# Graph attention on one core: batch 0's self_feat as seven block products, and the value blocks cleared and copied in two groups

## The chip, the core and the metric

The kernel runs on one core of a Trainium2 chip. The core has five engines with queues of their own: PE (TensorE; PEld are its weight loads), DVE (VectorE), ACT (ScalarE), POOL (GpSimd) and SP (SyncE, which here only issues DMAs; POOL and ACT issue a few as well). Each engine works through its instructions in the order in which they were written, and waits on semaphores for what the others have to deliver. The metric is the device time of one execution in microseconds (us). A difference of two kernels is told from runs on the same chip.

## The reference, cut to what matters

There are 16 batches of 512 rows with 512 features. Every row attends to the first 20 rows of its batch, with 16 heads, in two directions `d`:

```python
self_feat = concat([v, q_exp]) @ W_self.T + b_self          # q_exp is 0 where a row of v sums to 0
for d in range(2):
    A  = (adj if d == 0 else adj.swapaxes(1, 2))[:, :, :20, :]        # 11 labels
    vb = A @ w_bias + b_bias
    kv = self_feat[:, :20]
    qh, kh = self_feat @ Wq.T + bq, kv @ Wk.T + bk                    # 16 heads of 32
    aff = where(A.sum(-1) > 0, qh . kh / sqrt(32), -9e15) + vb
    out = out + (softmax(aff) @ kv) @ Wout + bout                     # per head
return v + relu(self_feat + out)
```

## The kernel before, in words

All numbers are fp32. Features lie on partitions (`C` = 4 chunks of 128), rows along the free dimension. The query projection is folded into the keys: `keys` computes `Wq` times the keys once, so that scores are self_feat times these folded keys. `Wout` is folded into the values in the same way by `values`.

**Setup** (lines 458 to 764). After the key projections (`key_rows`) come 22 bursts of `keys`. A burst is a group of matmuls into both buffers of the PSUM pool `ps_s`, which ACT (line 689) and DVE (line 691) evict into staging tiles `st`; SP writes these to `g_d` and `g1_d` in DRAM, and batch 0's part to `g0`. Between two bursts TensorE does one entry of `plan` (line 719), a filler: `v` and `w` are steps of `values`, `c` is `bias_scores`, `n` is `row_flags`, `s` a quarter pass of `self_feat(0, ...)`. Entry 0 follows burst 4, and so on. `values` ends with a copy by DVE and DMAs issued by POOL into `vw_d` (line 657). `bias_scores(0)` also has POOL clear a tile `c` (line 628) into which ACT then copies (line 630).

**self_feat.** For batches 1 to 15 it is built from 2 x 2 blocks with seven products instead of eight (`product`, line 249): POOL forms four sums of x (`x_sum`) and, once, four sums of the weights (`weight_sums`); DVE reads the partial accumulators (`partial`, line 284) into scratch tiles `u1` to `u3` and adds them to the other products (`joined`, line 297). Product n of batch b + 1 runs during batch b. Batch 0 uses the plain form: `self_feat(0, f, h)` makes one quarter, in eight steps, and `self_copy` adds the row flags times the query part. Three quarters are made in the setup; the last one, (1, 1), stands in tile 1 of batch 0 (line 873), ahead of that tile's scores.

**Main loop** (lines 786 to 984): 16 batches of four tiles `nt` of 128 rows. Per tile TensorE does `scores`. DVE does `weigh` (adds the mask terms of `full_add`, takes the maximum, subtracts), ACT the exponent (`expo`), DVE and POOL `normal`, DVE `turn` (a transpose). `full_add` and `x_sum` are POOL's. In tile 2 of the next batch `attend(b - 1)` multiplies the turned weights with the value blocks `vd`, and `finish` adds self_feat. The masks of batch b + 1 are made on the way: `mask_mul` on ACT (eleven activations), `mask_count` and `mask_sum` on DVE, `mask_spread` on ACT. `row_sum(b + 2, j)` on ACT sums the rows of x for the flags; `new_self(b + 1)`, a small ACT copy, opens the self_feat tile of the next batch. Both stand in tile 3.

**Value blocks.** `vd` must be block diagonal. So `clear_blocks` writes zeros over `bd_d` in DRAM with one DMA, in tile 1 of batch 0, and `blocks` copies the values of all 16 batches from `vw_d` into it with twelve DMAs, in tile 2 of batch 0. `load_values(b)` then reads one batch's block: batch 0's in tile 3 of batch 0, the others in tile 0 of the next batch.

**Order.** All of it is written out by hand (`manual_schedule`). SP's DMAs are one queue; `behind(dma, instruction)` makes one wait for an instruction of another engine, and those after it wait as well. A DMA also waits for the one eight places ahead of it, as they share eight semaphores.

Of the kernel before, what the change touches and what calls it, by code (L numbers as in the profile page):

```python
# [13 lines left out]
P = 128  # L14
# [4 lines left out]
def gat_kernel(  # L19
# [64 lines left out]
    vw_d = dram.tile([2, C, BM, P], F32, name="vw_d")  # L84
    bd_d = dram.tile([C, B, 32, HL, 2, DH], F32, name="bd_d")
# [5 lines left out]
    adds, fulls, wts, outs, held, sf_ps, conds, prods = {}, {}, {}, [], [None] * 3, {}, {}, {}  # L91
    sums, parts, us, done = {}, {}, {}, {}
# [42 lines left out]
    def load_values(b, ins=None):  # L135

        vds[b] = gp.tile([P, HL, 2, DH], F32, tag="vd", name=f"vd{b}", bufs=1)
        for c in range(C):
            behind(nc.sync.dma_start(
                vds[b][bass.ts(c, 32)].rearrange("p e i g -> p (e i g)"), bd_d[c, b].rearrange("r e i g -> r (e i g)")  # L140
            ), ins if c == 0 else None)

    def clear_blocks(zero):

        nc.sync.dma_start(
            bd_d.rearrange("c b r e i g -> (c b r) (e i g)").rearrange("(n p) w -> p n w", p=P),
            zero.unsqueeze(1).to_broadcast([P, C * B * 32 // P, HL * 2 * DH]),
        )

    def blocks():  # L150

        bb = bd_d.rearrange("c b r e i g -> (c b) r e i g")
        vv = vw_d.rearrange("d c (b m) (e g) -> d (c b) m e g", m=NG, e=HL)
        for e in range(HL):
            for i in range(2):
                j = (e * S) // 32 + i
                for d in range(2):
                    lo = max(e * S + d * NG, 32 * j)
                    hi = min(e * S + (d + 1) * NG, 32 * j + 32)
                    if lo < hi:  # L160
                        m, r = lo - e * S - d * NG, lo - 32 * j
                        nc.sync.dma_start(bb[:, r : r + hi - lo, e, i], vv[d, :, m : m + hi - lo, e])


# [29 lines left out]
    def self_feat(b, f, h, parts=((0, range(C)), (1, range(C)))):  # L194


        lo, hi = max(NG, h * N // 2), (h + 1) * N // 2
        for i, ks in parts:
            if (i, ks[0]) == (0, 0):
                if (f, h) == (0, 0):  # L200
                    new_self(b)
                held[0] = bank(f"ps_sf{b}_{f}{h}", 3 if (f, h) == (1, 1) else None)
            for k in ks:
                for a in range(HL):
                    nc.tensor.matmul(  # L205
                        held[0][bass.ts(a, R), i * N // 2 : i * N // 2 + hi - lo],
                        ws_v[:, k, bass.ds((2 * f + i) * P + a * R, R)], xs[b][:, k, lo:hi],
                        start=(k == 0), stop=(k == C - 1),
                    )
            if (i, ks[-1]) == (1, C - 1):  # L210
                sf_ps[b, f, h] = held[0]

    def self_copy(b, f, h):

        lo, hi = max(NG, h * N // 2), (h + 1) * N // 2
        ps = sf_ps.pop((b, f, h))
        for i in range(2):
            nc.vector.scalar_tensor_tensor(
                sfs[b][:, 2 * f + i, lo:hi], nzs[b][:, lo:hi], qw[:, 2 * f + i, b : b + 1],
                ps[:, i * N // 2 : i * N // 2 + hi - lo], ALU.mult, ALU.add,  # L220
            )

# [15 lines left out]
    def x_sum(b, n):  # L238

        t = sums[b, n] = xsum.tile([P, 2, HN], F32, tag=f"t{n}", name=f"t{b}_{n}")  # L240
# [8 lines left out]
    def product(b, n):  # L249
# [11 lines left out]
        if n == 1:  # L261
            parts[b, "a"] = [bank(f"ps_a{b}_{i}", i) for i in range(2)]
        if n == 2:
            parts[b, "d"] = bank(f"ps_d{b}", 2)
        if n == 5:
            parts[b, "c"] = bank(f"ps_c{b}", 3)
# [30 lines left out]
    def joined(b, n, key, f, l):  # L297
# [769 lines left out]
```

## Time and profile before

| | us |
|---|---|
| median of 3 runs | 587.78 (587.18 to 588.13) |
| profiled execution, its own time | 586.05 |
| its span, first to last instruction | 583.9 |
| PE busy, share of the span | 575.7 (99%) |
| DVE busy | 489.0 (84%) |
| ACT busy | 395.6 (68%) |
| POOL busy | 384.9 (66%) |

Setup is the time up to the first scores at 91.38 us; a batch in the middle of the loop takes some 30.5 us. In rows of the chain, numbers are the start, the length and the piece of work; in rows of a timeline, start, length, engine, line, operation, tiles and shapes, and in brackets the idle time of the engine ahead of it and what ended it ("issue": nothing that the profile shows). In the trace TensorE has two records for each matmul, so that 16 matmuls are "x32". Ends of matmuls are modelled. A row of a DMA is its issue on SP or POOL.

### The profile page before, as it was taken

The page shows a single profiled execution, that of the slowest core. Times are in us where ns is not written, and L with a number is a line of the kernel's source. Part 1 is how long each engine was busy: PE and PEld are TensorE (multiplying, and loading weights), DVE is VectorE, ACT ScalarE, POOL GpSimd, SP SyncE. Part 2 cuts the span into 40 slices and gives each one's busy share as a digit, 9 for nine tenths or more (in the row PEclk, how much of TensorE's full clock was granted, in tenths as well). Part 3 has the DMA queues.
Part 4 walks back from the last instruction along what each step waited for, and adds up shares of the span by engine and source line. Part 5 has one row for each costly group of instructions (what it writes and reads, how often), then busy time and mean ns, then how long its engine had stood idle before and what let it go on. Part 6 is the DMA issues. An engine that isn't in the chain of part 4 may idle for free.

```text
span 583.9 us, 30310 instructions
## 1 busy us (share of the span) xinstructions
PE 575.7 (99%) x13184; PEld 437.0 (75%) x13184; DVE 489.0 (84%) x783; ACT 395.6 (68%) x1162; POOL 384.9 (66%) x351
## 2 busy tenths in 40 slices
PE   9999999999999999999999999999999999999996
PEld 6654547887878787877878787787887878787873
DVE  0485565889898989899999999898989898989895
ACT  1334644586877777868686868687786877777671
POOL 2405663648778685858586777686868677776775
PEclk9999999999999999999999999999999999999999
DMA  8999899857766675757576767676676765664404
GB/s 303 388 407 311 331 377 320 273 123 213 209 197 196 185 214 169 217 167 217 168 214 171 214 171 212 177 199 188 199 202 187 199 198 172 199 199 114 144 15 146
DMA packets 103220, 124.14 MB, mean 213 GB/s; under 512 B 21712, under 2 KB 71920, under 8 KB 101040
## 3 DMA queue, kind: packets, MB, share of 16 engines
q1 hardware_dynamic: 101296, 119.79, 66.8%
q8 instruction: 104, 1.70, 1.3%
q0 software_dynamic: 672, 1.36, 1.0%
q10 hardware_dynamic: 1120, 1.06, 0.5%
q14 instruction: 28, 0.23, 0.2%
HBM read 82.30 MB, written 40.24 MB: 210 GB/s over the span
## 4 chain that ended last, share of the span: by engine, by line
PE 98%; DVE 0%; issue 0%; ACT 0%; DVEq 0%
PE ps_s L365 46%; PE ps_a L282 17%; PE ps_c L282 9%; PE ps_o L435 6%; PE ps_d L282 4%; PE ps_v L649 3%; PE ps_k L586 3%; PE ps_sf L205 2%; PE ps_kv L537 2%; PE ps_o L779 1%; PE ps_warm L496 1%; PE ps_nz L189 0%; PE ps_s L354 0%; PE ps_c L622 0%; PE ps_q L547 0%
## 5 line engine op out<-in xcount | busy, mean ns | idle before, releaser
L365 PEld LDWEIGHTS ps_s<-g,sf 128*32 128x32 f32 x8192 | 262.8, 110 | 20.9 <-issue 13.0
L365 PE MATMUL ps_s<-g,sf 128*32 128x152 f32 x8192 | 276.7, 293 | 0.5 <-ACT st L689 0.5
L337 ACT COPY both<-add 32x80 f32<-32x80 f32 x512 | 130.8, 256 | 53.8 <-DVE add L328 48.0
L417 POOL TENSOR_TENSOR s<-s,sm 128x640 f32<-128x640 f32 x63 | 80.4, 1276 | 94.2 <-DVE sm L416 68.2
L344 POOL TENSOR_TENSOR full<-cq,both 128x640 f32<-128x640 f32 x64 | 100.4, 1568 | 27.5 <-issue 21.3
L317 ACT ACTIVATE prod<-adj,wb_sb 128x80 f32<-128x80 int32 x330 | 112.4, 433 | 0.0
L392 ACT ACTIVATE s<-s 128x640 f32<-128x640 f32 x63 | 46.5, 738 | 64.1 <-DVE s L387 63.8
L449 POOL TENSOR_TENSOR o<-o,x 128x512 f32<-128x512 f32 x60 | 76.4, 1297 | 0.0
L379 DVE TENSOR_TENSOR full<-ps_s,full 128x608 f32<-128x608 f32 x63 | 48.8, 774 | 27.9 <-PE ps_s L365 22.6
L415 DVE TENSOR_REDUCE sm<-s 128x32 f32<-128x640 f32 x63 | 50.8, 806 | 9.5 <-ACT s L392 9.2
L282 PE MATMUL ps_a<-t,ws_s 128*32 128x246 f32 x960 | 55.4, 370 | 0.0
L383 DVE TENSOR_REDUCE ps_s<-full 128x32 f32<-128x640 f32 x63 | 52.2, 828 | 2.2
L424 DVE STREAM_TRANSPOSE wt<-s 128x640 f32<-128x640 f32 x63 | 52.7, 837 | 0.6 <-POOL s L417 0.6
L387 DVE TENSOR_TENSOR s<-full,ps_s 128x640 f32<-128x640 f32 x63 | 51.5, 817 | 1.1
L282 PEld LDWEIGHTS ps_a<-t,ws_s 128*32 128x32 f32 x960 | 31.6, 110 | 16.0
L328 DVE TENSOR_REDUCE add<-prod 128x80 f32<-128x960 f32 x32 | 36.8, 1150 | 6.2 <-ACT prod L317 4.4
L247 POOL TENSOR_TENSOR t<-x 128x492 f32<-128x492 f32 x30 | 34.6, 1153 | 9.5 <-DVE ps_s L383 5.4
L446 ACT ACTIVATE o<-o,bo 128x512 f32<-128x512 f32 x60 | 38.3, 713 | 0.6 <-DVE o L444 0.6
L435 PE MATMUL ps_o<-wt,vd 32*32 32x512 f32 (+5 forms) x816 | 36.7, 578 | 0.0
L444 DVE TENSOR_TENSOR o<-ps_o,sf 128x512 f32<-128x512 f32 x60 | 36.7, 668 | 0.0
L289 DVE SCALAR_TENSOR_TENSOR u<-nz,qw,ps_a 128x246 f32<-128x246 f32 x90 | 36.6, 448 | 0.0
L247 POOL TENSOR_TENSOR t<-x,t 128x492 f32<-128x492 f32 x30 | 34.5, 1150 | 2.3 <-DMA x<-in_xT 1.1
(239 smaller groups left out, 719.5 us busy)
## 6 DMA issues: line engine op xcount, KB each, us to landing
g_d<-st SPq DMA_DIRECT2D x16, 1064.0 KB, 5.9
g<-g_d SPq DMA_DIRECT2D x56, 304.0 KB, 3.6
out_T<-o SPq DMA_DIRECT2D x60, 256.0 KB, 3.3
x<-in_xT SPq DMA_DIRECT2D x56, 256.0 KB, 3.2
xn<-in_xn SPq DMA_DIRECT2D x52, 256.0 KB, 3.3
adj<-in_adj SPq DMA_DIRECT2D x56, 220.0 KB, 3.2
nz<-nz_d SPq DMA_DIRECT2D x14, 256.0 KB, 4.6
wk<-in_wkT SPq DMA_DIRECT2D x2, 1024.0 KB, 7.7
```

The costliest lines, as they stand in the source:

```text
L247: done["xsum"] = nc.gpsimd.tensor_sub(t, one, two)
L282: nc.tensor.matmul(to, lhs, x[:, k], start=start, stop=stop, skip_group_check=n != 2)
L317: nc.scalar.activation(p[:, :, l], a[:, :, l], AF.Identity, scale=wb_sb[:, l : l + 1])
L337: nc.scalar.copy(adds[b, h][bass.ts(a, R), :, g], add[r].rearrange("p (t m) -> p t m", t=2))
L344: done["full"] = nc.gpsimd.tensor_add(f, cqs[b].unsqueeze(1).to_broadcast(shape), adds[b, nt // 2][:, nt % 2].unsqueeze(2).to_broadcast(sh ...
L365: nc.tensor.matmul(to, sfs[b][:, k, bass.ds(nt * P + (2 * g + j) * R, R)], of, start=(onto is None and k == 0 and (whole or j == 0)), stop ...
L383: nc.vector.tensor_reduce(mx, f, AX.X, ALU.max)
L387: done["weigh"] = nc.vector.tensor_sub(s, f, mx.unsqueeze(3).to_broadcast(full))
L417: done["normal"] = nc.gpsimd.tensor_mul(s, s, sm.unsqueeze(3).to_broadcast(full))
L424: nc.vector.transpose(wts[b][:, nt], s.rearrange("p a h m -> p (a h m)"))
L435: nc.tensor.matmul(banks[a][bass.ds(at // 2 * DH, n * DH)].rearrange("p (t n) -> p t n", n=32), vd[r, bass.ds(at * DH, n * DH)], wt[r, :, ...
L449: nc.gpsimd.tensor_add(o[:, c], o[:, c], xs[b][:, c])
```

## The change

- `self_feat` and `self_copy` go. Batch 0 gets the seven products too, as fillers `p` of the last seven entries of `plan`, in the order 1, 2, 6, 7, 5, 4, 3, each with its `partial` or `joined`. Its four `x_sum` and the `weight_sums` stand ahead of them on POOL, in tiles of a free self_feat buffer. `plan` is rearranged: the `c` come two and one entries earlier and apart, all `v` are early, the four `w` apart.
- `partial` writes into the self_feat tile itself, and `joined` adds there; the scratch tiles go. `new_self(b + 1)` moves from tile 3 to tile 2, ahead of `weigh`.
- `vw_d` and `bd_d` are split into batches 0 and 1, and 2 to 15. `values` issues two DMAs instead of one for its first 128 rows.
- The first group is cleared by one DMA in tile 0 of batch 0 and copied by twelve small DMAs in tile 2 of batch 0, with loads for batch 1 between them. The second is cleared by eight DMAs (tile 3 of batch 0, and batch 1) and copied by twelve: two in batch 1, ten in batch 2. `load_values(0)` moves to tile 0 of batch 1.
- Loads of batch 1's masks, keys and constants, and of batch 2's `xn`, are issued in parts and later in batch 0; in batch 0, `row_sum(2, j)` moves from the head of tile 3 to behind `turn`.

```diff
-    vw_d = dram.tile([2, C, BM, P], F32, name="vw_d")
-    bd_d = dram.tile([C, B, 32, HL, 2, DH], F32, name="bd_d")
+    EARLY = 2
+    parts_of = ((0, EARLY), (EARLY, B))
+    vw_d = [dram.tile([2, C, (hi - lo) * NG, P], F32, name=f"vw_d{lo}") for lo, hi in parts_of]
+    bd_d = [dram.tile([C, hi - lo, 32, HL, 2, DH], F32, name=f"bd_d{lo}") for lo, hi in parts_of]
...
+    def clear_first(ins):
+        rows = EARLY * 32
+        behind(nc.sync.dma_start(
+            bd_d[0].rearrange("c b r e i g -> (b r) c (e i g)"),
+            zero[:rows].unsqueeze(1).to_broadcast([rows, C, HL * 2 * DH]),
+        ), ins)
+    def clear_rest(n, ins):
+        rows = (B - EARLY) * 8
+        to = bd_d[1][n // 2].rearrange("b r e i g -> (b r) (e i g)").rearrange("(n p) w -> p n w", p=rows)
+        behind(nc.sync.dma_start(
+            to[:, n % 2 * 2 : n % 2 * 2 + 2], zero[:rows].unsqueeze(1).to_broadcast([rows, 2, HL * 2 * DH])
+        ), ins)
...
-                        nc.sync.dma_start(bb[:, r : r + hi - lo, e, i], vv[d, :, m : m + hi - lo, e])
+                        found.append((bb[:, r : r + hi - lo, e, i], vv[d, :, m : m + hi - lo, e]))
+        return found
+    def spill(n):
+        for _ in range(n):
+            nc.sync.dma_start(*copies.pop(0))
...
-    def partial(b, n, f, l, to=None):
-        if to is None:
-            to = us[b, n] = xsum.tile([P, 2, HN], F32, tag=f"u{n}", name=f"u{b}_{n}")
+    def partial(b, f, l):
+        to = block(b, f, l)
...
                     for i, d in enumerate(ds):
-                        nc.gpsimd.dma_start(
-                            vw_d[d, :, bass.ds(t * P, rows)].rearrange("c r w -> r c w"),
...
+                        for n, lo, hi in ((0, 0, edge), (1, edge, rows)) if t == 0 else ((1, 0, rows),):
+                            nc.gpsimd.dma_start(
...
+            def block_product(n):
+                product(0, n)
+                f, args = {
+                    1: (partial, (0, 0, 0)), 2: (joined, (0, "d", 0, 0)), 6: (partial, (0, 0, 1)),
+                    7: (partial, (0, 1, 1)), 5: (joined, (0, "c", 1, 1)), 4: (partial, (0, 1, 0)),
+                    3: (joined, (0, "c", 0, 1)),
+                }[n]
+                f(*args)
...
-            plan = "bvv vv vv ccw vv ns ssss sssw vv vv ssss ssss vv vv nww ssss ssss".split()
+                "p": [(block_product, (n,)) for n in (1, 2, 6, 7, 5, 4, 3)],
+            plan = "bvv vvc vvc vvn vv vvw vv vv w w wn p p p p p p p".split()
...
+                if n == 9:
+                    row_sums(1)
+                    weight_sums()
                 if n == 11:
-                    row_sums(1)
-                if n == 13:
-                    weight_sums()
+                    new_self(0)
+                    for i in range(1, 5):
+                        x_sum(0, i)
...
-                    if b == 0:
-                        self_feat(0, 1, 1)
                     for g in range(2):
                         scores(b, nt, g, ps[g])
-                    if b == 0:
-                        self_copy(0, 1, 1)
...
                     normal(*prev)
+                    if b == 0:
+                        load_adj(1, 1, done["normal"], slice(0, 1))
+                        copies = blocks(0)
+                        spill(3)
+                        load_keys(1, range(1, 2))
+                        load_adj(1, 1, None, slice(1, 2))
+                        spill(3)
+                        load_keys(1, range(2, 3))
+                        spill(3)
+                        load_keys(1, range(3, C))
+                        spill(3)
+                        load_xn(2, 1, None, slice(0, 1))
...
                         product(b + 1, 2)
+                        new_self(b + 1)
...
                 if nt == 3 and more:
                     mask_count(b + 1, 0)
                     product(b + 1, 6)
-                    new_self(b + 1)
...
-                    if b + 2 < B:
+                    if 0 < b < B - 2:
                         for j in range(4):
                             row_sum(b + 2, j)
                     normal(*prev)
+                    if b == 0:
+                        load_xn(2, 1, done["xsum"], slice(1, 2))
+                        clear_rest(0, done["normal"])
...
                     turn(*prev)
...
+                    if b == 0:
+                        clear_rest(1, done["mixed"])
+                        for j in range(4):
+                            row_sum(2, j)
                     if b + 2 < B:
                         load_x(b + 2, range(1), done["weigh"])
                         load_x(b + 2, range(1, 2), done["exp"])
+                        if b in (1, 2):
+                            spill(2)
```

More of the change, by code (lines that the diff above doesn't have):

```diff
@@ L191, in row_flags @@
         nc.vector.tensor_scalar(nzs[b], ps[:, :N], 0.0, None, ALU.not_equal)
[L194 to L221, printed above, removed]
     def weight_sums():
@@ L238, in x_sum @@
     def x_sum(b, n):
-        t = sums[b, n] = xsum.tile([P, 2, HN], F32, tag=f"t{n}", name=f"t{b}_{n}")
+        if b > 0:
+            t = xsum.tile([P, 2, HN], F32, tag=f"t{n}", name=f"t{b}_{n}")
+        else:
+            if n == 1:
+                held[0] = sfp.tile([P, C, N], F32, tag="sf", name="t0")
+            t = held[0][:, n - 1, : 2 * HN].rearrange("p (k n) -> p k n", k=2)
+        sums[b, n] = t
         one, two = {
@@ L261, in product @@
         if n == 1:
-            parts[b, "a"] = [bank(f"ps_a{b}_{i}", i) for i in range(2)]
+            parts[b, "a"] = [bank(f"ps_a{b}_{i}", i if b else None) for i in range(2)]
         if n == 2:
-            parts[b, "d"] = bank(f"ps_d{b}", 2)
+            parts[b, "d"] = bank(f"ps_d{b}", 2 if b else None)
         if n == 5:
-            parts[b, "c"] = bank(f"ps_c{b}", 3)
+            parts[b, "c"] = bank(f"ps_c{b}", 3 if b else None)
         for i in range(2):
@@ L336, in mask_spread @@
                 r = bass.ts(g, R)
-                nc.scalar.copy(adds[b, h][bass.ts(a, R), :, g], add[r].rearrange("p (t m) -> p t m", t=2))
+                done["spread"] = nc.scalar.copy(adds[b, h][bass.ts(a, R), :, g], add[r].rearrange("p (t m) -> p t m", t=2))
     def full_add(b, nt):
@@ L781, in put_self @@
             )
+        gs[0] = g0
         prev = None
@@ L831, in gat_kernel @@
                             load_x(b + 1, range(3, C), done["normal"])
+                        if b == 1:
+                            clear_rest(2, done["partial"])
                         for g in range(2):
@@ L917, in gat_kernel @@
                         product(b + 1, 2)
-                    s = weigh(b, nt, pair, (lambda: partial(b + 1, 1, 0, 0)) if more else None)
+                        new_self(b + 1)
+                    s = weigh(b, nt, pair, (lambda: partial(b + 1, 0, 0)) if more else None)
                     expo(s)
```

98 lines of the change are left out of this document (53 added, 45 removed).

## The prediction

> **What bounds the kernel.** I read the page's chain first, then the chain in order of time with its shares by line, the windows, and then the timelines of single engines up to 145 us, where the change ends.
>
> ```profile
> span 583.9 us, 30310 instructions
> ...
> PE 98%; DVE 0%; issue 0%; ACT 0%; DVEq 0%
> ```
>
> ```profile
> 152.80:183.30 30.50, 30.50 (x792) 24.24 (x788) 27.84 (x44) 23.52 (x72) 22.08 (x20) 1.00 0.67 195
> ```
>
> ```profile
> 41.50:91.38 49.88, 49.36 (x524) 23.71 (x522) 30.19 (x57) 23.29 (x55) 29.48 (x34) 1.00 0.94 343
> ```
>
> (Stretch, its length, then busy time of PE, PEld, DVE, ACT and POOL, the granted clock, DMA share and GB/s.) TensorE is the chain. A batch in the steady loop takes 30.5 us without a gap, so a change gains only by taking matmuls out or by closing one of the few gaps before 145 us; everything else can only open gaps. Those gaps lie here:
>
> ```profile
> 54.30 0.33 PE ps_g(1, 2, 1, 1, 2)0_523 L674 x2
> ...
> 55.29 1.05 PE ps_nz L189 x2
> 56.34 0.54 PE ps_sf L205 x8
> ...
> 58.27 1.73 PE ps_sf L205 x32
> ...
> 62.32 1.01 PE ps_v L649 x4
> ```
>
> ```profile
> 64.76 1.91 PE ps_v L649 x4
> ...
> 95.72 3.45 PE ps_sf L205 x64
> ...
> 111.70 1.66 PE ps_a L282 x32
> 113.36 4.13 PE ps_s L365 x128
> ...
> 132.41 2.17 PE ps_o L435 x48
> ...
> 142.17 1.66 PE ps_a L282 x32
> ```
>
> ```profile
> 91.38 4.34 PE L365 MATMUL ps_s<-g,sf 128*32 128x152 f32 x128 [0.52 <-ACT st L689]
> ...
> 110.24 1.45 PE L282 MATMUL ps_d<-x,ws_v 128*32 128x246 f32 x24 [0.73 <-issue]
> ```
>
> A burst of `keys` takes 0.99 (54.30 to 55.29). Two are stretched: 56.88 (56.34 + 0.54) to 58.27 is 1.39, and 63.33 to 64.76 is 1.43, 0.4 lost each. The first scores lose 0.52, product 2 of batch 1 loses 0.73.
>
> **The sum, in the setup.** The old self_feat is 2.4% of the chain, 14.0 us:
>
> ```profile
> by line: PE ps_s L365 45.7%; PE ps_a L282 17.1%; PE ps_c L282 8.5%; PE ps_o L435 6.1%; PE ps_d L282 4.3%; PE ps_v L649 3.3%; PE ps_k L586 3.1%; PE ps_sf L205 2.4%; PE ps_kv L537 1.7%; PE ps_o L779 0.7%; PE ps_warm L496 0.6%; PE ps_nz L189 0
> ```
>
> It is eight passes of 16 matmuls. A product is one pass of 246 columns: 1.66 in the loop (111.70), and between bursts about 1.80, scaling the 1.73 of 236 columns at 58.27. Seven cost 12.6 at the dearer price, which I take because they stand between bursts: -1.4 (to -2.4 at 1.66). The two `c` and the four `w` steps stand apart now and pay the change of tile layout more often: +0.2, estimated from 62.32 (1.01 for a `w`, where two together need less than twice that).
>
> The last burst is followed by product 3 instead of the scores, so its eviction is covered: -0.5. In DVE's timeline a mask reduction stands right ahead of the eviction of each stretched burst; the new plan has longer fillers there, so the reduction has passed: -0.85.
>
> New gaps in the setup come from three places.
>
> ```profile
> 52.48 1.17 DVE L691 TENSOR_SCALAR st<-ps_g(1, 2, 0, 0, 2)1_501 128x608 f32<-128x608 f32 x2 [1.98 <-PE ps_g(1, 2, 0, 0, 2)1_501 L674]
> ```
>
> ```profile
> 46.39 0.99 POOL L657 DMA_DIRECT2D vw_d<-v  x1 [16.69 <-DVE v L655]
> 47.38 0.66 POOL L628 MEMSET c<- 128x640 f32 x1
> ```
>
> - Two bursts are followed by a lone `w` of 1.01. A burst needs both `ps_s` buffers back, and the eviction takes 1.17 plus some 0.1 at each end: 0.4 late, twice, +0.8 (0 if the buffers free by halves; 1.0 if it adds 0.1 more each).
> - Bias scores 0 now run two bursts earlier, right behind the first `v`. ACT's copy into `c` must wait for POOL's memset, which stands behind the `vw_d` DMAs of that `v`, two of them now: 46.39 + 0.99 + 0.66 = 48.0 with one, 48.4 to 49.0 with two. ACT evicts in order behind that copy. The burst to evict ends near 46.9 (the `v` done at 45.3, `c` 0.6, burst 1.0), so its eviction runs near 49 to 50.2 where 47 to 48 was due. TensorE's filler (two `v` and a `c`, 2.5) lasts to 49.4: +0.75 (0 to 1).
> - The second mask count comes behind a `joined` in the filler of product 2, ahead of an eviction, as in the two stretched bursts that lost 0.4: +0.25, between 0 and 0.4, since this filler (1.80) is longer than one of those two (1.05 + 0.54) and shorter than the other.
>
> The other POOL work (`row_sums`, `weight_sums`, four `x_sum`) ends well ahead of products 6 and 7, which need it. If it slipped past them, a product would wait by as much. Setup: -0.75.
>
> **The sum, batches 0 and 1.** Taking 3.45 out of batch 0 does not make DVE, ACT and POOL faster. Count from S, the start of the first scores (91.59 = 95.72 - 4.13, with 4.13 per scores pass).
>
> ```profile
> 100.63 1.27 POOL L417 TENSOR_TENSOR s<-s,sm 128x640 f32<-128x640 f32 x1 [2.02 <-DVE sm L416]
> ...
> 104.17 1.57 POOL L344 TENSOR_TENSOR full<-cq,both 128x640 f32<-128x640 f32 x1
> ```
>
> ```profile
> 107.87 0.73 DVE L379 TENSOR_TENSOR full<-ps_s,full 128x608 f32<-128x608 f32 x1
> ...
> 109.37 0.84 DVE L289 SCALAR_TENSOR_TENSOR u<-nz,qw,ps_a 128x246 f32<-128x246 f32 x2
> ...
> 114.92 1.15 DVE L328 TENSOR_REDUCE add<-prod 128x80 f32<-128x960 f32 x1
> ...
> 125.29 1.15 DVE L328 TENSOR_REDUCE add<-prod 128x80 f32<-128x960 f32 x1 [0.31 <-ACT prod L317]
> ...
> 129.10 0.84 DVE L424 STREAM_TRANSPOSE wt<-s 128x640 f32<-128x640 f32 x1
> ```
>
> ```profile
> 111.77 0.63 ACT L169 ACTIVATE xn<-xn 128x512 f32<-128x512 f32 x1
> ...
> 114.14 0.19 ACT L169 ACTIVATION_READ_ACCUMULATOR xn<-xn 128x1 f32 x1
> 116.10 4.27 ACT L337 COPY both<-add 32x80 f32<-32x80 f32 x16 [1.78 <-DVE add L328]
> 120.78 0.74 ACT L392 ACTIVATE s<-s 128x640 f32<-128x640 f32 x1 [0.41 <-DVE s L387]
> 121.42 3.77 ACT L317 ACTIVATE prod<-adj,wb_sb 128x80 f32<-128x80 int32 x11
> ```
>
> - POOL's `full_add(0, 2)` ended at S + 14.15 before and does so again. Then DVE's `weigh` starts at S + 14.2, its `partial` 1.50 later (107.87 to 109.37), whose first half is out 0.42 later: product 6 can start at S + 16.25. TensorE is there at S + 15.7 (three passes of 4.13, two products of 1.66): a gap of 0.55 in the place of the 0.73. Net -0.2.
> - The four row sums of batch 2 (111.77 to 114.33, 2.56) leave an idle ACT and now stand behind the exponent. Chain: mask sum at S + 21.25 (7.05 after `weigh`), spread from S + 22.4 to 26.7, exponent 0.64, row sums 2.56, mask product 3.77: S + 33.7. DVE's mask sum, `weigh` and transpose wait for it: the transpose of batch 0's last tile starts 3.6 after the mask sum (125.29 to 129.10 less 0.2 of waiting) and ends at S + 38.2. `attend(0)` reads it. TensorE is there 20.7 after product 6 (111.70 to 132.41): S + 36.95. +1.35 (0 if DVE regains its lag; ACT alone shifts by 2.56, and 2.4 of slack stood between 129.94 and 132.41).
>
> ```profile
> 132.54 0.79 DVE L379 TENSOR_TENSOR full<-ps_s,full 128x608 f32<-128x608 f32 x1 [0.94 <-PE ps_s L365]
> ...
> 140.69 0.84 DVE L289 SCALAR_TENSOR_TENSOR u<-nz,qw,ps_a 128x246 f32<-128x246 f32 x2
> ```
>
> - DVE then needs 9.8 from that transpose to the `partial` in front of batch 2's product 6 (129.94 to 140.69 less the 0.94), TensorE 9.75 from `attend` (132.41 to 142.17): +0.5. After that DVE's idle time takes up the lag.
>
> The DMAs: clears and the second group's copies move to batches 0 to 2, where the DMA share has room (0.67), keys and masks of batch 1 are issued later, and `load_values(2)` waits for the last two copies. I cost them at nothing on the strength of this:
>
> ```profile
> 108.64 11.93 SPq L162 DMA_DIRECT2D bd_d<-vw_d  x12
> ```
>
> ```profile
> L139 SPq DMA_DIRECT2D vd<-bd_d x64: 303/413/1957, 124.7 to 563.0; - x64
> L162 SPq DMA_DIRECT2D bd_d<-vw_d x12: 611/716/1692, 108.6 to 119.9; - x12
> ```
>
> ```profile
> xn<-in_xn SPq DMA_DIRECT2D x52, 256.0 KB, 3.3
> ```
>
> Between `normal(0, 1)` (S + 15.3) and batch 2's last `xn` SP has 18 issues, 12 of them copies of an eighth of the rows. At 0.65 a copy (near the least of the 12) and 0.45 a load (0.41 is the median of the `vd` loads) they take 10.5, so that `xn` is issued by S + 25.8 and lands 3.3 later near S + 29, when ACT comes to it. If it is late, ACT's row sums wait, and all behind them. `new_self` one tile earlier and `partial` written straight into `sf` keep their lengths; the relus and reductions ahead cover the 0.24 copy, and uncovered it would cost that 15 times.
>
> Together -0.75 - 0.2 + 1.35 + 0.5 = +0.9. The sum is made on the profiled execution (586.05, span 583.9); the median of the runs, 587.78, is 1.7 above it and takes the same difference: 588.7.
>
> **Rivals.** B, the new gaps do not come: `ps_s` frees by halves, POOL is quick, DVE regains its lag. Then the 0.8, 0.75, 1.35 and 0.5 fall away: -2.5, 585.3. For it: the chain shows TensorE waiting for almost nothing over 584 us. Against: ACT's 2.56 has 2.4 of slack at most. C, the copies stay slow: at 1.0 each as before (11.93 for 12) the last `xn` lands near S + 33, 4 late, and `attend(0)` with it: +4.5, 592.3. It decides as soon as a copy takes over 0.7. For it: SP waits for older DMAs before it issues more. Against: each copy has an eighth of the rows. [...] D, the setup is bound by DMA (0.94 share in the window above): closer bursts find their staging tiles still being written out, +1.5 on top, 590.2.
>
> **How the numbers follow.** Forecast 0.45, B 0.22, C 0.20, D 0.13. I call 0.2% (1.2 us) the bound of a difference that can be told. The forecast's own range is 587.3 to 590.0: of its 0.45, 0.31 is no change, 0.10 slower, 0.04 faster. B gives 0.20 faster and 0.02 the same; C and D are slower. So 0.24, 0.33 and 0.43. The range reaches into B and C until some 0.2 is left outside, 585.6 to 592.2.
>
> **What would show it.** Right: seven products of 1.7 to 1.8 in the setup, gaps of 0.4 behind the lone `w`, a late ACT eviction near 50 us, no wait at the first scores, a gap before product 6 in batch 0, and one over 1 us before `attend(0)` that ends with DVE's transpose. Wrong: `attend(0)` on time (B), ACT waiting for `xn` near S + 30 (C), evictions waiting for DMA (D), or a gap in every later batch, which I do not expect.

## The result, and the profile after

| | before | after |
|---|---|---|
| median of 6 runs each | 587.48 (586.50 to 589.34) | 593.11 (591.84 to 596.86) |
| profiled execution, its own time | 586.05 | 592.69 |
| its span | 583.9 | 590.9 |

The changed kernel is slower: ratio 1.0106 [1.0083, 1.0128], 5.6 us between the medians. Here and below a ratio is worked out from the single executions, so that it can differ a little from the quotient of the two medians (1.0096 here). The forecast was 588.7 with a range up to 592.2.

The page's span, and its chain by engine:

```profile
span 590.9 us, 30299 instructions
...
PE 86%; DMA 4%; DVE 3%; ACT 3%; issue 1%; POOL 1%; SPq 0%; DVEq 0%; ACTq 0%
```

Before, PE was 98% of the chain and DMA was not on it. TensorE's timeline of the changed kernel, the rows of `attend` and the rows with a wait of over 0.5:

```profile
50.77 0.40 PE L669 MATMUL ps_g(1, 1, 0, 1, 2)0_480<-khD,wq_sb 32*128 32x152 f32 x2 [0.60 <-ACT st L684]
...
134.31 4.08 PE L428 MATMUL ps_o<-wt,vd 32*32 32x512 f32 x48 [2.41 <-DVE wt L417]
...
166.90 3.98 PE L428 MATMUL ps_o<-wt,vd 32*32 32x512 f32 x48 [0.21 <-DMA vd<-bd_d]
...
199.53 3.57 PE L428 MATMUL ps_o<-wt,vd 32*32 32x512 f32 x48
...
231.34 2.24 PE L428 MATMUL ps_o<-wt,vd 32*32 32x512 f32 x48
```

`attend` takes 2.24 in these rows where nothing disturbs it (2.17 in rows of the chain). In the kernel before, the second and the third were these:

```profile
162.82 2.24 PE L435 MATMUL ps_o<-wt,vd 32*32 32x512 f32 x48
...
193.29 2.58 PE L435 MATMUL ps_o<-wt,vd 32*32 32x512 f32 x48
```

In the changed kernel the first three take 4.08, 3.98 and 3.57. Laid beside the rows of before (first scores 91.59, `attend` at 132.41, 162.82, 193.29 and 224.11), the span's 7.0 us come apart like this; S is the start of the first scores, 94.61 here, and the predicted column has the terms of the prediction's sum:

| stretch | before | after | difference | predicted |
|---|---|---|---|---|
| start to the first `v` (ahead of the change) | 40.48 | 41.09 | +0.6 | 0 |
| first `v` to S | 51.1 | 53.5 | +2.4 | +2.7 |
| S to `attend(0)` | 40.82 | 39.70 | -1.1 | -2.3 |
| `attend(0)` itself | 2.17 | 4.08 | +1.9 | 0 |
| to `attend(1)` | 28.2 | 28.5 | +0.3 | +0.5 |
| `attend(1)` | 2.24 | 3.98 | +1.7 | 0 |
| to `attend(2)` | 28.2 | 28.7 | +0.4 | 0 |
| `attend(2)` | 2.58 | 3.57 | +1.0 | 0 |
| from there on | | | 0 | 0 |

(The predicted +2.7 is 3.45 less 0.75, and -2.3 is -3.45 + 1.35 - 0.2.) The first stretch differs from run to run by as much: the first `v` stood between 39.90 and 41.55 in the profiles below, whatever the kernel.

SP's timeline (x2 or x3: so many issues in one row) and ACT's, where they bear on this:

```profile
110.39 2.22 SPq L180 DMA_DIRECT2D bd_d<-vw_d  x3
...
118.91 1.94 SPq L180 DMA_DIRECT2D bd_d<-vw_d  x3
120.90 0.94 SPq L113 DMA_DIRECT2D xn<-in_xn  x2
...
157.82 1.83 SPq L180 DMA_DIRECT2D bd_d<-vw_d  x2
...
162.60 1.76 SPq L141 DMA_DIRECT2D vd<-bd_d  x4
...
171.90 2.94 SPq L180 DMA_DIRECT2D bd_d<-vw_d  x3
...
190.24 1.60 SPq L180 DMA_DIRECT2D bd_d<-vw_d  x2
...
195.94 3.42 SPq L141 DMA_DIRECT2D vd<-bd_d  x4
```

```profile
124.76 0.63 ACT L186 ACTIVATE xn<-xn 128x512 f32<-128x512 f32 x1 [1.42 <-DMA xn<-in_xn]
...
182.47 0.63 ACT L186 ACTIVATE xn<-xn 128x512 f32<-128x512 f32 x1 [2.59 <-DMA xn<-in_xn]
```

The last `xn` of batch 2 stands behind the twelve copies, and ACT waits 1.42 for it. In batch 1 the values are issued at 162.60, behind two copies (157.82), 4.3 us ahead of the `attend` that needs all four parts; in batch 2 they are issued behind two copies again (190.24), whose results they read, and at 195.94, after SP stood idle for 2.2 us, which fits that those have to land first. That is 3.6 us ahead of their `attend`. In the kernel before it was 6.8 and 6.1 us:

```profile
156.05 2.48 SPq L139 DMA_DIRECT2D vd<-bd_d  x4
...
187.24 1.77 SPq L139 DMA_DIRECT2D vd<-bd_d  x4
```

The chain in order of time of the changed kernel runs through the values in batch 1, and through a late `xn` in batch 2:

```profile
162.60 4.17 DMA vd<-bd_d
166.77 0.14 issue
166.90 3.98 PE ps_o L428 x48
...
179.62 3.86 DMA xn<-in_xn
```

In batch 0 a clear stands on that chain as well: POOL's first `x_sum` waited 8.78 us, by the profile for the first group's clear, and began at S + 8.0 instead of S + 6.0. It cost nothing there, since POOL's `full_add(0, 2)` ended at S + 14.2, as before.

### The profile page after: what moved, and what is told of

It reads as the page before. It is cut to its first block, busy times and chain, and to the rows that moved or that the text cites. A ratio compares the mean times of both kernels' runs of the same rounds, so it can differ in the third digit from the quotient of the medians.

```text
span 590.9 us, 30299 instructions
## 1 busy us (share of the span) xinstructions
PE 579.6 (98%) x13152; PEld 437.5 (74%) x13152; DVE 492.3 (83%) x786; ACT 395.4 (67%) x1162; POOL 390.9 (66%) x357
## 4 chain that ended last, share of the span: by engine, by line
PE 86%; DMA 4%; DVE 3%; ACT 3%; issue 1%; POOL 1%; SPq 0%; DVEq 0%; ACTq 0%
PE ps_s L358 40%; PE ps_a L276 16%; PE ps_c L276 8%; PE ps_o L428 7%; PE ps_d L276 4%; PE ps_k L579 3%; PE ps_v L642 3%; ACT both L330 1%; DMA ws_q<-in_wsT 1%; DMA bd_d<-zero 1%; PE ps_kv L530 1%; DMA vd<-bd_d 1%; PE ps_o L776 1%; DMA xn<-in_xn 1%; ACT prod L310 1%
## 5 line engine op out<-in xcount | busy, mean ns | idle before, releaser
L358 PEld LDWEIGHTS ps_s<-g,sf 128*32 128x32 f32 x8192 | 262.4, 110 | 22.2 <-issue 14.2
L330 ACT COPY both<-add 32x80 f32<-32x80 f32 x512 | 130.8, 256 | 59.3 <-DVE add L321 53.5
L276 PE MATMUL ps_a<-t,ws_s 128*32 128x246 f32 x1024 | 59.2, 371 | 0.0
L282 DVE SCALAR_TENSOR_TENSOR sf<-nz,qw,ps_a 128x246 f32<-128x246 f32 x128 | 51.5, 443 | 0.4 <-PE ps_a L276 0.4
L276 PEld LDWEIGHTS ps_a<-t,ws_s 128*32 128x32 f32 x1024 | 33.3, 110 | 17.8 <-issue 0.9
L428 PE MATMUL ps_o<-wt,vd 32*32 32x512 f32 (+5 forms) x816 | 41.4, 602 | 2.6 <-DVE wt L417 2.4
L241 POOL TENSOR_TENSOR t<-x 128x492 f32<-128x492 f32 x32 | 36.7, 1148 | 10.3 <-DMA bd_d<-zero 8.8
L439 ACT ACTIVATE o<-o,bo 128x512 f32<-128x512 f32 x60 | 38.2, 709 | 0.6 <-DVE o L437 0.6
L241 POOL TENSOR_TENSOR t<-x,t 128x492 f32<-128x492 f32 x32 | 36.8, 1148 | 1.3
```

The costliest lines, as they stand in the source:

```text
L241: done["xsum"] = nc.gpsimd.tensor_sub(t, one, two)
L276: nc.tensor.matmul(to, lhs, x[:, k], start=start, stop=stop, skip_group_check=n != 2)
L282: done["partial"] = nc.vector.scalar_tensor_tensor(to[:, i], nzs[b][:, half(l)], qw[:, 2 * f + i, b : b + 1], parts[b, "a"][i][:, :HN], AL ...
L330: done["spread"] = nc.scalar.copy(adds[b, h][bass.ts(a, R), :, g], add[r].rearrange("p (t m) -> p t m", t=2))
L358: nc.tensor.matmul(to, sfs[b][:, k, bass.ds(nt * P + (2 * g + j) * R, R)], of, start=(onto is None and k == 0 and (whole or j == 0)), stop ...
L428: nc.tensor.matmul(banks[a][bass.ds(at // 2 * DH, n * DH)].rearrange("p (t n) -> p t n", n=32), vd[r, bass.ds(at * DH, n * DH)], wt[r, :, ...
```

## The experiments

Theory at the start: the setup went as predicted; the loss has two sources, the wait before `attend(0)` with what follows it, and loads that come late because clears and copies stand ahead of them in SP's queue. Rivals: the products themselves open gaps; the transfers, not their order, are too much; `attend(0)` is long for want of values. All ratios are to the kernel before, run on the same chip.

### Each part alone

First part alone: products and plan as changed, one group of value blocks, cleared, copied and loaded where the kernel before has it, row sums at the head of tile 3.

```diff
-    EARLY = 2
-    parts_of = ((0, EARLY), (EARLY, B))
+    parts_of = ((0, B),)
...
+                if b == 0 and nt == 1:
+                    load_adj(1, 0)
+                    load_cq(1)
+                    clear_blocks(zero)
+                    load_adj(1, 1)
+                    load_xn(2, 0)
+                    load_xn(2, 1)
+                if b == 0 and nt == 2:
+                    copies = blocks(0)
+                    spill(12)
```

> The first part of the change alone: the seven products in the setup, the new plan, partial into the self_feat tile; value blocks, loads and row sums as in the kernel before. Theory (the loss is all in the value blocks' DMAs and the moved row sums): the first scores come 2.4 to 2.7 later and batch 0 is 3.45 shorter, so 1 us faster than the kernel before, 586.5, with no low clock at attend(0). Rival (taking the product quarter out of batch 0 alone leaves attend(0) waiting for DVE, ACT and POOL): a gap of 1 us or more before attend(0), 588 or above.

585.72, ratio 0.9979 [0.9960, 0.9997]. Run again:

> The first part alone once more, unaltered, beside the run with the late clear: 0.9979 of the kernel before, as measured, and the two stops in batch 0.

586.47, 0.9978 [0.9967, 0.9989]. So the first part gains some 1.3 us, near the 1 us of the theory. TensorE's rows with a wait, and `attend`, of the first of the two runs:

```profile
105.08 2.12 PE L348 MATMUL ps_s<-g,sf 128*32 128x152 f32 x57 [1.55 <-issue]
...
111.84 1.65 PE L266 MATMUL ps_a<-t,ws_s 128*32 128x246 f32 x26 [1.02 <-issue]
...
132.68 2.24 PE L418 MATMUL ps_o<-wt,vd 32*32 32x512 f32 x48
...
163.30 2.24 PE L418 MATMUL ps_o<-wt,vd 32*32 32x512 f32 x48
```

There is no wait before `attend(0)`, and `attend` is 2.24 long in batches 0, 1 and 2. S comes 0.9 earlier after the first `v` than in the changed kernel (52.45 against 53.33, each to the first row of the scores), and the wait of 0.60 at 50.77 is missing: with undivided `vw_d`, POOL issues one DMA there, not two. There are two stops in batch 0 that no semaphore explains; the late clear, below, was to test them.

Second part alone: everything but the products and the plan, so that tile 1 of batch 0 has its quarter of self_feat.

```diff
-            plan = "bvv vvc vvc vvn vv vvw vv vv w w wn p p p p p p p".split()
+            plan = "bvv vv vv ccw vv ns ssss sssw vv vv ssss ssss vv vv nww ssss ssss".split()
...
+                    if b == 0:
+                        self_feat(0, 1, 1)
                     for g in range(2):
                         scores(b, nt, g, ps[g])
+                    if b == 0:
+                        self_copy(0, 1, 1)
```

> The second part of the change alone: value blocks in two groups, with all loads, clears, copies and row sums where the changed kernel has them, but batch 0's self_feat by the plain quarters and the old plan, so that tile 1 of batch 0 keeps its 3.45 of TensorE work. Theory (the late DVE and ACT in front of attend(0) are covered by those 3.45, the late value loads of batches 1 and 2 are not): no wait and no low clock at attend(0), attend(1) and attend(2) still 1.0 to 1.8 long: 3 to 3.5 above the kernel before, 590.5 to 591. Rival (the second part has its whole price by itself): 593 or more.

594.09, 1.0116 [1.0085, 1.0146]: the rival. The second part has its whole price by itself; 1.0116 and 0.9978 make 1.0094 together, against 1.0106 measured. The 3.45 of TensorE work that was to cover the late DVE and ACT covered nothing:

```profile
136.57 4.04 PE L458 MATMUL ps_o<-wt,vd 32*32 32x512 f32 x48 [4.11 <-DVE wt L447]
168.85 2.94 PE L458 MATMUL ps_o<-wt,vd 32*32 32x512 f32 x48
194.01 2.40 PE L388 MATMUL ps_s<-g,sf 128*32 128x152 f32 x64 [1.78 <-DVE sf L312]
```

Work that TensorE does in tile 1 also holds back the scores that DVE has to take ahead of the mask sum (116.00 here, 115.99 in the changed kernel, though S is 2.2 earlier), and ACT waited 1.92 and 1.70 for the two last `xn`.

### The long attend(0), and the wait ahead of it

```diff
+                        if b == 1:
+                            for _ in range(2):
+                                nc.tensor.matmul(banks[0], ws_v[:, 0, :P], ws_v[:, 0], start=True, stop=True)
                         attend(b - 1, banks)
```

> The changed kernel with two matmuls of 512 columns (about 1 us each) put in front of attend(0), into a bank that attend overwrites; nothing else moves. They fill most of the 2.41 us for which TensorE idles there. Theory (the idle time lowers the granted clock, to 0.50 from 135 to 137 us, and that alone makes attend(0) 4.08 long instead of 2.17): attend(0) is about 2.2 again and the kernel 1.8 faster than the changed kernel, 591.3 against 593.1. Rival (attend(0) is long because parts of its value blocks come late, and the low clock only goes with it): attend(0) stays near 4, no difference.

One stretch of the windows (after the length, busy time of five engines; the last three columns are granted clock, DMA share and GB/s), of the changed kernel and then of this one, and this one's `attend(0)`:

```profile
135.00:136.00 1.00, 1.00 (x32) 0.08 (x15) 0.97 (x3) 0.95 (x5) 0.00 (x0) 0.50 0.86 295
```

```profile
135.00:136.00 1.00, 1.00 (x37) 0.25 (x16) 0.97 (x3) 0.95 (x5) 0.16 (x1) 1.00 0.96 305
```

```profile
134.09 2.75 PE L428 MATMUL ps_o<-wt,vd 32*32 32x512 f32 x48 [0.97 <-DVE wt L417]
```

With the gap filled the granted clock stays 1.00, and `attend(0)` takes 2.75 instead of 4.08: 1.3 of the 1.9 was the half clock. But the kernel was no faster, 594.33, 1.0136 [1.0114, 1.0157]. Counted from the first `v`, `attend(0)` ended 1.0 earlier than in the changed kernel (96.26 against 97.30), `attend(2)` 0.7, `attend(3)` 0.3: the later ones, which need their values, gave it back (`attend(1)` 4.19 long, `attend(3)` 2.68). So the mechanism held, and the gain of 1.8 that I expected of it did not come.

Then `xn` ahead of batch 0's copies:

```diff
                         copies = blocks(0)
+                        load_xn(2, 1, None, slice(0, 1))
+                        load_xn(2, 1, None, slice(1, 2))
                         spill(3)
```

> The changed kernel with both halves of batch 2's last xn load issued ahead of the twelve copies of batch 0 instead of behind them. Theory (ACT waits 1.42 for that load because SP has the copies ahead of it, and the wait goes straight into attend(0)): the wait in front of attend(0) falls from 2.41 to about 1.0; if so short an idle time does not lower the clock, attend(0) is 2.2 again: -3.3, 589.8; if it does, -1.4, 591.7. Rival (the load is slow because the DMA engines are busy, not because of its place): ACT still waits, 593.

```profile
133.07 2.82 PE L428 MATMUL ps_o<-wt,vd 32*32 32x512 f32 x48 [0.50 <-DMA vd<-bd_d]
...
190.22 2.40 PE L358 MATMUL ps_s<-g,sf 128*32 128x152 f32 x64 [1.88 <-DVE sf L282]
```

DVE's transpose in front of `attend(0)`, in the changed kernel and then in this one:

```profile
133.37 0.84 DVE L417 STREAM_TRANSPOSE wt<-s 128x640 f32<-128x640 f32 x1
```

```profile
131.71 0.84 DVE L417 STREAM_TRANSPOSE wt<-s 128x640 f32<-128x640 f32 x1
```

591.76, 1.0095 [1.0074, 1.0116]. In batch 0 ACT no longer waits for `xn`, the transpose ends at S + 38.0 instead of S + 39.6, and the wait before `attend(0)` falls to 0.50, so the load's place was the cause; what the wait now ends with is the values. `attend(0)` takes 2.82 behind it instead of 4.08. Counted from the first `v`, `attend(0)` ended 2.6 earlier than in the changed kernel (94.70 against 97.30); half of it was given back in batch 2, where ACT waited 0.88, 2.80 and 0.91 for its `xn` and TensorE 1.88 for what stands behind it (the granted clock was 1.00 in the 4 us behind those 1.88). So 589.8 was not reached.

### The copies of the second group

```diff
-                        if b in (1, 2):
-                            spill(2)
...
+                        if b == 1:
+                            spill(2)
+                        if b == 2:
+                            spill(4)
```

(in tile 2 behind the `xn` loads; of the other six, two each in tiles 0, 1 and 3 of batch 2.)

> The changed kernel with the twelve copies of the second group at other places of SP's queue: 2 in tile 2 of batch 1, and in batch 2 two in tile 0, two in tile 1, four in tile 2 behind the xn loads and two in tile 3 ahead of the x loads; none stands ahead of value loads or xn loads any more. Theory (attend(1) and attend(2) are long, 3.98 and 3.50, because vd lands late behind copies in SP's queue, and ACT waits 2.9 for xn for the same reason): both are 2.2 to 2.5 again and the kernel is 3 us faster than the changed one, 590. Rival (the DMA engines are too busy in batch 2, wherever the copies stand): less than 1 us is gained.

```profile
133.46 3.60 PE L428 MATMUL ps_o<-wt,vd 32*32 32x512 f32 x48 [2.94 <-DVE wt L417]
...
165.97 2.24 PE L428 MATMUL ps_o<-wt,vd 32*32 32x512 f32 x48
...
196.44 2.24 PE L428 MATMUL ps_o<-wt,vd 32*32 32x512 f32 x48
```

589.67, 1.0067 [1.0045, 1.0089]. `attend(1)` and `attend(2)` are 2.24 again: they were long because copies stood ahead of their values. Counted from the first `v`, `attend(3)` ends 3.2 earlier than in the changed kernel, as the theory said. The ratios, 1.0067 against 1.0106, make the gain 2.3 us, with intervals that just overlap; the changed kernel was not run on this chip, so that the two medians can't be held against each other.

### Both, and where the waits go then

The changed kernel once more, on the chip of the next three:

> The changed kernel once more, unaltered, on the chip of the three that follow, so that they have a changed kernel to be held against: 593, the ratio near 1.011.

593.06, 1.0109 [1.0082, 1.0136]. The copies moved, and the row sums behind batch 1's mask product (e6):

```diff
                         mask_mul(b, 1)
+                        if b == 1:
+                            for j in range(4):
+                                row_sum(2, j)
```

> The changed kernel with the second group's copies at the places of the run before that moved them, and in addition the four row sums of batch 2 on ACT behind the mask product of batch 1 instead of ahead of it (its flag's store goes behind the value loads for that reason). Theory (what is left of the loss is the wait of 2.4 to 2.9 before attend(0), made by the row sums and their late load, and the half clock behind it, some 1.5): no wait before attend(0), clock 1.00, attend(0) near 2.3, so 4.3 less than the run that moved the copies alone: 585.4. Rival (ACT's 2.56 is only moved, and makes the exponent of batch 1's first tile late instead): a new wait of 1 to 2.5 in tile 1 of batch 1, 587 to 588.

```profile
133.44 2.80 PE L428 MATMUL ps_o<-wt,vd 32*32 32x512 f32 x48 [1.63 <-DMA vd<-bd_d]
...
195.27 3.51 PE L428 MATMUL ps_o<-wt,vd 32*32 32x512 f32 x48
```

588.87, 1.0022 [1.0002, 1.0042], 4.2 less than the changed kernel beside it. DVE is in time (its transpose ends at S + 35.6), but now `attend(0)` waits 1.63 for its values, and `attend(2)` is long again: neither theory nor rival. With `xn` first and the copies moved:

> The changed kernel with both moves of DMAs, the xn load ahead of batch 0's copies and the second group's copies moved, and the row sums left where the change put them. Theory: ACT waits for no xn load in batches 0 and 2, the wait before attend(0) is 0.5 to 1.0 and does not lower the clock, attend(0) 2.3 to 2.8: 3.4 less than with the copies alone, 586.3. If the row sums' place were the whole cause and the load did not matter, the wait would stay near 2.4 and the time near 589.7.

588.43, 1.0019 [1.0000, 1.0037], not the 586.3 of the theory. In its profiled execution (591.12, the longest of its eleven) `attend(0)` has no wait of its own (2.68 long), three stops of TensorE that no semaphore explains add up to 2.61, and `attend(2)` waits 1.13 for values. And e6 with another plan in the setup:

```diff
-            plan = "bvv vvc vvc vvn vv vvw vv vv w w wn p p p p p p p".split()
+            plan = "bvv vvc vvc vn vv vv vv vv vw ww wn p p p p p p p".split()
```

> The kernel with the copies and the row sums moved, and in addition the plan of the setup changed so that no burst is followed by a single step of values: bvv vvc vvc vn vv vv vv vv vw ww wn and then the seven products. Theory (each lone step of the changed kernel stretches the burst behind it by 0.4, and ACT's late copy behind it): the first scores come 0.8 earlier than with both moved, 584.6. Rival (the burst is stretched by the mask work on ACT at that time, whatever the filler): within 0.3 of the run with both moved.

588.94, 1.0041 [1.0018, 1.0064]. S stands 53.27 behind the first `v`, against 53.15: the number of the rival, but not its reason. The bursts behind `w` steps now take 0.9 to 1.0 instead of 1.4, so the lone `w` did stretch them. What that saves is lost again at another burst, the one behind the first product, which takes 1.9 instead of 0.9. DVE comes late to evict there, after it stood 1.99 for a DMA of `values` (DVE's row, then TensorE's):

```profile
75.72 0.69 DVE L648 COPY v<-ps_v 128x512 f32<-128x512 f32 x1 [1.99 <-DMA vw_d<-v]
```

```profile
78.23 0.53 PE L669 MATMUL ps_g(3, 0, 0, 0, 2)1_745<-khD,wq_sb 32*128 32x304 f32 x2 [0.22 <-DVE st L686]
```

(Its profiled execution, 593.38, is the longest of its eleven; `attend(0)` waits 3.63 for its values in it.)

Next, on top of e6, batch 0's values issued in tile 3 of batch 0 already (e9); then the copies spread otherwise (e10), `xn` first with the row sums in the change's place (e11), and the second group's twelve copies left out (e12).

```diff
                         load_x(b + 2, range(1, 2), done["exp"])
+                        if b == 0:
+                            load_values(0)
```

> The run with copies and row sums moved, and in addition batch 0's value loads issued in tile 3 of batch 0, behind the x loads, instead of behind three more loads and clears in tile 0 of batch 1. Theory (with ACT's part gone, the value loads became the last thing attend(0) waits for, 1.63, and made it 2.80 long): no wait before attend(0), 2.24 long, so 2.2 less than that run. Rival (the value loads wait for the copies ahead of them to land, or the DMA engines are full, so that an earlier issue lands no earlier): the wait stays.

For e10 (the two of tile 0 and the two of tile 1 as in e9):

```diff
                         if b == 1:
-                            spill(2)
+                            spill(4)
...
                             load_keys(b + 1, range(3, C), done["normal"])
-                        if b == 2:
-                            spill(2)
```

> As the run before it in this call, and the second group's copies once more elsewhere: four in tile 2 of batch 1, and in batch 2 two in tile 0, two in tile 1, four in tile 2, none in tile 3. Theory (attend(2) was 3.51 long because the last copies held up x loads and value loads behind them): attend(2) 2.24, 1.3 less than the run before. Rival (the copies must be paid somewhere): the loss turns up at attend(1) or in ACT's wait for xn.

> As the run before, but with the row sums of batch 2 where the change put them and the xn load ahead of batch 0's copies. Theory: the row sums themselves still make DVE's transpose late, a wait of about 0.5 to 1.0 before attend(0), so 0.5 to 1.0 slower than the run before; this is the 1.35 that the prediction gave them, without the late loads. If the row sums cost nothing without the late loads, the two are equal.

> As the spread copies, but with the twelve copies of the second group left out, so that batches 2 to 15 attend to value blocks of zeros; only the time is of interest. It bounds what the copies still cost where they were spread. Theory (it was their place in SP's queue): within 0.5 of the spread copies. Rival (their transfers take DMA time that the loads need, wherever they stand): 1 us or more faster.

TensorE in e9, and then SP:

```profile
131.90 2.24 PE L428 MATMUL ps_o<-wt,vd 32*32 32x512 f32 x48
...
157.68 0.47 PE L358 MATMUL ps_s<-g,sf 128*32 128x152 f32 x8 [1.50 <-DMA g<-g_d]
158.64 2.02 PE L358 MATMUL ps_s<-g,sf 128*32 128x152 f32 x56 [0.49 <-DMA g<-g_d]
```

```profile
147.12 1.78 SPq L180 DMA_DIRECT2D bd_d<-vw_d  x2
148.95 1.76 SPq L135 DMA_DIRECT2D g<-g_d  x2
```

In e9 and e10 `attend(0)` has no wait and is 2.24 long, as the theory said, and `attend(1)` and `attend(2)` are 2.24 as well. Yet the times of e9, e10 and e11 are 590.11 (1.0039 [1.0016, 1.0061]), 589.63 (1.0045 [1.0028, 1.0062]) and 590.30 (1.0039 [1.0019, 1.0060]), no better than e6: now the keys of batch 2, issued behind copies (at 148.95 in e9), come late, 1.50 + 0.49 in e9, 3.04 in four waits in e10, 2.03 in e11. That was e10's rival, with another load than it named. What e10 was to mend, the long `attend(2)`, was gone in e9 already, where the copies stand as in e6; so the place of the last copies alone did not make it. The times of e11 and e10 are not told apart, so what the row sums' place costs is not shown by them; in e11's trace DVE's transpose ended at S + 38.0 and TensorE waited 0.84 before `attend(0)`, as its theory said.

Without the copies, e12: 587.44, 1.0003 [0.9979, 1.0027], and TensorE waits for no load in batches 1 and 2. The rival: spread as they were, the copies still cost some 2 us. The products alone are at 0.9978, so by the ratios some 1.5 us are left for the clears, the first group and the moved loads. That is not clear of the noise, and no run takes these apart. In this trace TensorE has one stop left:

```profile
137.15 4.47 PE L358 MATMUL ps_s<-g,sf 128*32 128x152 f32 x80 [2.13 <-issue]
```

```profile
138.00:139.00 1.00, 1.00 (x23) 1.00 (x19) 0.00 (x0) 1.00 (x4) 0.95 (x1) 0.50 0.79 238
```

The stop stands inside a pass of scores, and the granted clock is 0.50 behind it (the second row is of the windows).

### A late clear

First part alone, the large clear behind the loads:

```diff
-                    clear_blocks(zero)
                     load_adj(1, 1)
                     load_xn(2, 0)
                     load_xn(2, 1)
+                    clear_blocks(zero)
```

> The first part alone, with the one large clear issued behind batch 1's masks and batch 2's xn instead of ahead of them. Theory (with the clear ahead, ACT waited 1.65 for xn and TensorE stopped 1.55 and 1.02 in tiles 2 and 3 of batch 0 while the DMA engines were full): ACT does not wait, the two stops fall below 0.5 each, and the time is 1.5 below the first part alone. Rival (the stops have nothing to do with the clear): equal within 0.4.

SP, and then TensorE:

```profile
106.15 0.38 SPq L146 DMA_DIRECT2D bd_d<-zero  x1
115.97 10.61 SPq L170 DMA_DIRECT2D bd_d<-vw_d  x12
130.91 2.69 SPq L140 DMA_DIRECT2D vd<-bd_d  x4
```

```profile
133.54 3.80 PE L418 MATMUL ps_o<-wt,vd 32*32 32x512 f32 x48 [1.37 <-DMA vd<-bd_d]
```

589.40, 1.0025 [1.0010, 1.0040], 3 us worse than the first part alone on the same chip. ACT no longer waits for `xn`, but the stops remain (1.11 and 0.29, against 1.49 and 0.23 in the run beside it), so the clear's place is not their cause. And SP goes on only 9.4 us after the clear, with the copies that write into what it clears, and the values follow those: the wait has moved to `attend(0)` once more.

## Why the prediction was wrong

- **Setup, -0.75: right.** S came 2.4 later after the first `v`, which is -1.0 beside the 3.45 saved. The seven products took 1.80 each, ACT's late eviction cost 0.60 at 50.77 and its burst another 0.1, and it goes with the second `vw_d` DMA (first part alone). The bursts behind two lone `w` took 1.4 each, and the burst that follows the second mask count 0.2 more than the others, where the sum has 0.25. With no lone `w` the first went away and the setup was no shorter, because another burst became late.
- **Product 6 of batch 0: right in time, partly by luck.** It began at S + 16.4 (forecast 16.25), but with no gap in front of it in this trace: TensorE itself came 0.7 later than the S + 15.7 of the forecast, 0.24 of it in a stop within the scores. (The -0.2 should have been -0.4 by the prediction's own figures: 16.25 against 20.1 less 3.45.) Product 6 of batch 2, +0.5: did not come, since TensorE was late by more than DVE.
- **Row sums, `attend(0)` +1.35: right but for the load.** DVE's transpose ended at S + 39.6 where 38.2 was forecast, and the wait was 2.41. The missing 1.4 is ACT's wait of 1.42 for `xn`: with that load in time the transpose ended at S + 38.0 (`xn` first, and e11); with the row sums moved behind the mask product it ended at S + 35.6 (e6). The load was issued at S + 26.3 (forecast S + 25.8) but landed for ACT at S + 30.1, not S + 29.
- **"The DMAs ... I cost them at nothing": the step that failed.** I followed SP's queue through batch 0 alone. In batches 1 and 2 the copies stand ahead of value and `xn` loads, so that the values are issued 4.3 and 3.6 us ahead of their `attend` instead of 6.8 and 6.1: +1.7, +1.0 and +0.4 there (with the copies moved `attend(3)` ended 3.2 earlier), and 1.4 of the wait before `attend(0)`. I had counted "room" by the DMA share of 0.67, an average; what decided in these runs was the one load that was due next. After moving each load that was late, the next one was: values of batch 0, then keys of batch 2. Twelve copies cost some 2 us even where they were spread (589.63 against 587.44). How much of that is their place in the queue and how much their transfers stays open.
- **Not in the sum: the clock.** The wait of 2.41 was followed by a granted clock of 0.50 for 3.4 us, which is 1.3 of the 1.9 that `attend(0)` took longer (4.08, against 2.75 in the run with the gap filled). So 1.35 turned into some 4.
- **Rivals.** C has nearly the time (592.3), which is mostly luck, as its road is only in part the one that was taken. The late `xn` did come, but by 1.4 instead of 4, and a copy took 0.65 to 0.74 in batch 0 (2.22 for three, 1.94 for three; 0.68 on average), just below the 0.7 from which I let it decide. The rest is batches 1 and 2. B and D did not come.

What the copies cost each, the trace tells by their sizes, one row for either group from the list of DMA issues, beside SP's rows above:

```profile
bd_d<-vw_d SPq DMA_DIRECT2D x4, 140.0 KB
...
bd_d<-vw_d SPq DMA_DIRECT2D x4, 20.0 KB
```

By SP's rows a copy of the second group (28 to 140 KB) held SP for 0.80 to 0.98, one of the first (4 to 20 KB) for 0.65 to 0.74: a seventh of the bytes at over two thirds of the price. In this trace, then, the price hardly fell with the bytes. But the greater part of the loss came from the larger copies of the second group, by their place ahead of other loads.

## What to carry to other kernels

Transfers that move into a busy period are not free because the engines have room on average (the DMA share was 0.67 in a batch of the kernel before, and the second part alone ran at 1.0116): list the loads behind them in their queue, with what each has to spare, and cost the one that is due first. When taking one wait away brings out another of the same kind, as most of the rearrangements did here, there may be no room left in that stretch, and the work has to go elsewhere: here the version that beats both kernels takes the products alone (0.9978) and leaves the value blocks as they were. And a wait of TensorE over 2 us cost more than its length here: behind the 2.41 of the changed kernel the granted clock was 0.50 for 3.4 us, and `attend(0)` took 4.08, against 2.75 with the gap filled.

## What the runs showed of the hardware

**The clock.** Idle times of TensorE and the granted clock behind them, from the windows of the runs: 2.13 (the second group's copies left out), 2.24 (the changed kernel run again, in batch 2), 2.41 (the changed kernel), 2.94 (the second group's copies moved), 3.63 (e8) and 4.11 (the second part alone) were each followed by 0.50 for some 3.4 us (5.0 at least after the 3.63), and so were 0.52 and 1.67 with 1.2 of work between them (the changed kernel run again, before `attend(0)`). After 1.50 (e9), 1.55 (the first part alone), 1.63 (e6), 1.75 (e11) and 1.88 (`xn` first) it stayed at 1.00. So of these single waits the longest with 1.00 behind it was 1.88, and the shortest with 0.50 behind it 2.13.

**Stops without a releaser.** Inside passes of scores or products TensorE stopped for 1.0 to 2.1 us with nothing that the profile shows: 1.55, 1.02 and 1.49 in the first part alone, 2.13 without copies; the kernel before had one of 0.73. In the windows of 1.6 to 3.0 us that hold those over 1.1 us the DMA share was 0.86 to 1.08, but in the 2.6 us that hold one of 1.03 us (e7) it was 0.58, and in the 1.9 us that hold one of 0.46 us (`xn` first) 0.03. They differ between executions of one kernel (2.57 and 1.72 in two of the first part alone). Their cause stays open; the one run meant for it only showed that it is not the place of the large clear.
